# Seven products in place of eight for layer 2's first keys and queries, earlier inversions in layer 0, and a weight load from two queues

## The chip, the core and the metric

The kernel runs on one core of one Trainium2 chip. The metric is the device time of one execution in microseconds (us). Before the change it is 2660.78 us, the median of three runs (2659.78 to 2661.41). The profiled execution took 2661.49 us, its trace spans 2659.6 us, and TensorE was granted 0.999 of its full clock over that span.

PE below is TensorE's matmul pipe, DVE is VectorE, ACT is ScalarE, POOL is GpSimd, SP is the engine that issues most DMAs. All engines run at once; each works through its own list of instructions, and an instruction waits until the tiles that it reads and the buffers that it writes are free.

## What is computed

Four layers are applied one after the other to `x` of shape (4, 512, 64, 64), in float32. The four images are independent. Cut to what matters here:

```python
# layer 0: attention over all 4096 positions of one image, 64 channels
t = einsum('oc,bchw->bohw', w_qkv, x)           # key, query, value: 64 channels each
attn = softmax(einsum('bdk,bdq->bkq', key, query), axis=1)
x = scale * einsum('oc,bchw->bohw', w_out, einsum('bdk,bkq->bdq', value, attn)) + x
# layer 1: 1x1, 3x3 and 1x1 convolutions; weights mixed from 8 experts by a router; ReLUs; residual
# layer 2: linear attention
Q = softplus(Wq x + bq);  K = softplus(Wk x + bk);  V = Wv x + bv     # Q, K: 64 channels
KV = einsum('bmn,bcn->bmc', K, V)
norm = 1 / einsum('bnm,bm->bn', Q, K.sum(-1) + 1e-6)
x = x + gamma * einsum('bnm,bmc,bn->bcn', Q, KV, norm)
# layer 3: project to 1024 channels; the second half is scanned along rows and columns,
# goes through a sigmoid and gates the first half; residual
```

## The kernel before

An image's 4096 positions are held as four "pairs" of 1024 positions, and a pair as four chunks of 128 channels; `x[p, c, n]` is one pair. `P` is 128, `NB` 512, `KC` 4, `NPAIR` 4, `D` 64, `NT` 32, `ROUND` 8, `RING` 12. PE follows the program's order throughout. DVE and ACT follow it inside `manual_schedule` blocks that name them; elsewhere a scheduler orders them when the program is built.

PSUM is given out by two tags: three buffers of 128x1024 (`pair_psum`) and two of 128x512 (`bank`). A product that asks for a buffer waits until the last reader of the buffer's old content is done.

```python
def pair_psum(name):
    return ps.tile([P, 2, NB], F32, tag="s", name=name, bufs=3)
def bank(name, shape=(P, NB)):
    return ps.tile(list(shape), F32, tag="acc", name=name)          # 2 buffers
```

Start: the weights of layer 0 come in one transfer on ACT's queue, the first image in 16 transfers of 512 KB on SP's queue. The projections of layer 0 already use Strassen's seven products; the first image has a step list of its own:

```python
nc.scalar.dma_start(wqkv_sb, wqkv_t)
...
if b == 0:
    first = ("zero v0:0 1:0 v0:1 1:1 seed v0:2 2:0 v0:3 2:1 c11 t5 v1:0 v1:1 5 t6 v1:2 v1:3 cp01 t7 6 e2 "
             "v2:0 v2:1 t4 7 e3 c22 tr01 n5 4 c21 n6 3 c12 n7 v2:2 v2:3 n4")
# a digit: that product; v: values; t, n: sums on DVE; c11: four copies of keys on ACT
```

Layer 0's attention. In each of 16 rounds PE makes eight score tiles `s`, ACT takes their exponentials, DVE adds them up in `acc`, and PE multiplies eight earlier ones with the values. When a pair of queries is through, PE sums `acc` over partitions (`den`), DVE inverts it, and four output products `y` follow, one in a round:

```python
def inverse_sums(pr):
    den = bank(...);  2 matmuls of ones with accs[pr]
    recs[pr] = block(...);  nc.vector.reciprocal(recs[pr], den)
def sums(pr, early=True):
    if early: inverse_sums(pr)
    o = avs[pr] * recs[pr]                     # DVE
    if early: sum_range(pr)                    # two reductions on DVE
def out_step(pr, m):                           # y = pair_psum(...), 2 matmuls; x += scale * y on DVE
    add_out(pr, m, out_product(pr, m))

for g in range(NPAIR * NT // ROUND):
    for i in range(g * ROUND, (g + 1) * ROUND):
        scores(i)
    ...
    while done < (g + 1) * ROUND - (RING - ROUND):
        if done == NPAIR * NT - 5:
            inverse_sums(NPAIR - 1)            # the last pair, ahead of its last values
        pr = values(done)
        done += 1
        if pr is not None:
            late.append((g, lambda pr=pr: sums(pr)))
            if pr < NPAIR - 2:
                late += [(g + 1, lambda pr=pr, m=m: out_step(pr, m)) for m in range(KC)]
    ...
    if late and late[0][0] <= g:
        late.pop(0)[1]()                       # one step of the waiting list in a round
```

Layer 1's last convolutions run into layer 2's first features:

```python
def conv3(pr, h2):
    for m in range(KC):
        y = pair_psum(f"c3_{b}_{pr}_{m}")
        for h in range(2):
            nc.tensor.matmul(y[:, h, :], wc[:, KC + 9 + m, :], h2[:, h, :], start=True, stop=True)
        xm = xs[pr][:, m, :]
        nc.vector.scalar_tensor_tensor(xm, flat(y), bn_s[:, 2 + m:3 + m], xm, ALU.mult, ALU.add)
        nc.scalar.activation(xm, xm, AF.Relu, bias=bn_t[:, 2 + m:3 + m])

def features(w, pair):                         # w = 1: keys, 0: queries; 16 matmuls of 64 columns
    z = pair_psum(f"z_{b}_{w}_{pair[0]}")
    for i in range(2):
        feature_part(w, pair, z, i, 0, KC)
    return lambda: softplus(w, pair, z)

def softplus(w, pair, z, in_parts=False):
    nc.scalar.activation(e, z, AF.Abs, ...)
    nc.scalar.activation(pos, z, AF.Relu, ...)
    nc.scalar.activation(e, e, AF.Exp, scale=-1.0)
    nc.vector.tensor_scalar(u, e, 1.0, None, ALU.add)
    nc.scalar.activation(ln, u, AF.Ln)         # then softplus_end:
    # DVE: u = (u - 1) - e;  pos = pos + ln;  two times k = pos - u (or q)

h2[2] = conv2(2)
conv3(1, h2[1])
h2[3] = conv2(3)
weights = load_quarters(b)
features(1, (0, 1))()()
conv3(2, h2[2])
...
rest = features(0, (0, 1))
with tc.manual_schedule(engines={mybir.EngineType.DVE}):
    key_transpose((0, 1))
    rest = rest()
    move(0, 0)                                 # xtr, by pair_psum; its copy on DVE
    move_by_halves(0, 1)
    conv3(3, h2[3])
    g = bank(f"g_{b}", (P, C))
    keys = features(1, (2, 3))
    rest()
    ...
```

Layer 3 works through step lists that interleave "s" (the half that is scanned), "g" and "h" (gates). The last image ends with a list of its own, in which `rows`, `columns`, `fourth`, `second` are DVE's, and `turn`, `sigmoid`, `copy_out`, `third`, `d` are ACT's:

```python
end_steps = (...,
    ("s7", "s copy_out 3", "l turn 0", "l columns 0", "l sigmoid 1"), ("s5", "s fourth"),
    ("s4", "s third", "d", "s rows 1", "l sigmoid 0"), ("g5",),
    ("s3", "s second", "s turn 1", "s rows 0"), ...,
    ("g7", "s sigmoid 1", "g copy_out 3", "g first", "g fourth"), ("h6", "h copy_out 2"),
    ("h2", "s sigmoid 0", "h first"), ...)
```

Of the kernel before, what the change touches and what calls it, by code (L numbers as in the profile page):

```python
# [8 lines left out]
F32 = mybir.dt.float32  # L9
AF = mybir.ActivationFunctionType  # L10
ALU = mybir.AluOpType
# [35 lines left out]
def unshifted(ctx: ExitStack, tc: tile.TileContext, fits, x, wqkv_t, wout_t, router_t,  # L47
# [13 lines left out]
# [4 lines that stand above are left out]
        return ps.tile(list(shape), F32, tag="acc", name=name)  # L65
# [4 lines left out]
    def block(name, shape=(P, NB)):  # L70
        return blkp.tile(list(shape), F32, tag="blk", name=name)
# [25 lines left out]


    wqkv_sb = const.tile([P, KC, 3 * D], F32, tag="wqkv", name="wqkv_sb")
    nc.scalar.dma_start(wqkv_sb, wqkv_t)  # L100
    prm_sb = const.tile([P, NPRM], F32, tag="prm", name="prm_sb")
    nc.scalar.dma_start(prm_sb, prm)
    def col(i, n=1):
# [109 lines left out]
    class Projections:  # L213
# [16 lines left out]
        def steps(self, b):  # L230
            first = "v1 cp01 5 1 seed v2a t6 2 c11 t4 n5 6 v2b e2 n6 7 e3 c22 tr01 n7 4 c21 3 c12 n4"
            if b == 0:

                first = ("zero v0:0 1:0 v0:1 1:1 seed v0:2 2:0 v0:3 2:1 c11 t5 v1:0 v1:1 5 t6 v1:2 v1:3 cp01 t7 6 e2 "
                         "v2:0 v2:1 t4 7 e3 c22 tr01 n5 4 c21 n6 3 c12 n7 v2:2 v2:3 n4")
            return first.split(), "5 1 seed v3a 2 c11 6 v3b e2 cp23 7 e3 c22 tr23 k 4 c21 3 c12".split()

# [109 lines left out]
    def layer0(b, xs, pro):  # L347
# [62 lines left out]
        def sums(pr, early=True):  # L410
            if early:
                inverse_sums(pr)
            av, rec = avs[pr], recs[pr]
            o = block(f"o_{b}_{pr}")
            if pr >= NPAIR - 2:
                i = pr - NPAIR + 2
                nc.vector.scalar_tensor_tensor(o, av, 1.0, rec, ALU.mult, ALU.mult, accum_out=osum[:, i:i + 1])
            else:
                nc.vector.tensor_tensor(o, av, rec, ALU.mult)
            outs[pr] = o  # L420
            if early:
                sum_range(pr)
# [31 lines left out]
        with tc.manual_schedule(engines={mybir.EngineType.Activation}):  # L454
# [3 lines that stand above are left out]
                if 1 < g < 2 + 2 * KC:  # L458
                    pool(NPAIR - 2 + (g - 2) // KC, (g - 2) % KC)
                if g == 1:  # L460
                    pro.key_copies()
                while done < (g + 1) * ROUND - (RING - ROUND):
                    if done == NPAIR * NT - 5:
                        inverse_sums(NPAIR - 1)
                    pr = values(done)
                    done += 1
                    if pr is not None:
                        late.append((g, lambda pr=pr: sums(pr)))
                        if pr < NPAIR - 2:
                            late += [(g + 1, lambda pr=pr, m=m: out_step(pr, m)) for m in range(KC)]  # L470
                if b == 0 and g == 1:
                    router = router_of_values()
                if b == 0 and g == 2:
                    router()
                if late and late[0][0] <= g:
                    late.pop(0)[1]()
        assert not late
# [61 lines left out]
    def layer1(b, xs, wcq, sel, rw, ex4, ex7):  # L539
# [98 lines left out]
                                     AF.Relu, bias=bn_t[:, 1:2], scale=bn_s[:, 1:2])  # L638
            return h2

        def conv3(pr, h2):
            for m in range(KC):
                y = pair_psum(f"c3_{b}_{pr}_{m}")
                for h in range(2):
                    nc.tensor.matmul(y[:, h, :], wc[:, KC + 9 + m, :], h2[:, h, :], start=True, stop=True)  # L645
# [3 lines that stand above are left out]
# [9 lines left out]
    def layer2(b, xs, sums_of_six, mix_last, conv2, conv3, wcq, qs):  # L658
# [14 lines left out]
        def features(w, pair):  # L673
# [4 lines that stand above are left out]
# [27 lines left out]
        def key_transpose(pair):  # L705
            ktr = pair_psum(f"ktr_{b}_{pair[0]}")
            for i, pr in enumerate(pair):
                for j in range(TPB):
                    nc.tensor.transpose(ktr[:, i, j * P:(j + 1) * P], kts[1, pr][:, j * P:(j + 1) * P], ident)
            kt = four(f"kt_{b}_{pair[0]}")  # L710
            nc.vector.tensor_copy(kt, ktr)
            for i, pr in enumerate(pair):
                kts[pr] = kt[:, i, :].rearrange("p (j c) -> p j c", c=P)
# [40 lines left out]
        with tc.manual_schedule(engines={mybir.EngineType.DVE}):  # L754
            sums_of_six(0)
            sums_of_six(1)
            sums_of_six(2)
            mix_last()
            h2 = {0: conv2(0)}
            sums_of_six(3)  # L760
            h2[1] = conv2(1)
            conv3(0, h2[0])
        h2[2] = conv2(2)
        conv3(1, h2[1])
        h2[3] = conv2(3)
        weights = load_quarters(b)
        features(1, (0, 1))()()
        conv3(2, h2[2])


        def invert(pair):
# [14 lines left out]
            q = qs[:, pair[0]:pair[1] + 1, :]  # L786
            nc.vector.tensor_tensor(q, q, nrm, ALU.mult)

        rest = features(0, (0, 1))
        with tc.manual_schedule(engines={mybir.EngineType.DVE}):  # L790
            key_transpose((0, 1))
            rest = rest()
            move(0, 0)
            move_by_halves(0, 1)
            conv3(3, h2[3])
            g = bank(f"g_{b}", (P, C))
            keys = features(1, (2, 3))
            rest()
            keys = keys()
            products(0, ahead(1))  # L800
            keys()
            products(1, ahead(2))
            kfold = bank(f"kfold_{b}", (P, NPAIR))
            nc.tensor.matmul(kfold, fold, ks, start=True, stop=True)
            ksum = small.tile([P, 1], F32, tag="ksum", name=f"ksum_{b}")
            nc.vector.tensor_reduce(ksum, kfold, AX.X, ALU.add)
            for h in range(2):
                r = slice(h * D, (h + 1) * D)
                nc.vector.tensor_scalar(kbd[r, 16 * h:16 * (h + 1)], ones[r, 0:16], ksum[r, :], 1e-6, ALU.mult, ALU.add)
            key_transpose((2, 3))  # L810
            inv = invert((0, 1))
            products(2, ahead(3))
            divide((0, 1), inv)
            weights[2]()
            products(3)
            g_sb = block(f"gsb_{b}", (P, C))
            nc.scalar.copy(g_sb, g)
            gt = block(f"gt_{b}", (P, KC, P))

            late = (0, (2, 3), pair_psum(f"z_{b}_0_2"))  # L820
            feature_part(*late, 0, 0, 2)

            gk = pair_psum(f"gk_{b}")
            for kc in range(KC):
                nc.tensor.matmul(gk[:, 0, kc * P:(kc + 1) * P], g_sb[:, kc * P:(kc + 1) * P], fold,
                                 start=True, stop=True)
            nc.scalar.copy(gt, gk[:, 0, :].rearrange("p (kc c) -> p kc c", c=P))
            feature_part(*late, 0, 2, 2)
            kv = small.tile([P, C], F32, tag="kv", name=f"kv_{b}", bufs=1)
            for i in range(2):  # L830
                part = slice(i * C // 2, (i + 1) * C // 2)
                kvp = bank(f"kvp_{b}_{i}", (P, C // 2))
                for kc in range(KC):
                    nc.tensor.matmul(kvp, gt[:, kc, :], wv_sb[:, kc, part], start=kc == 0, stop=kc == KC - 1)
                nc.vector.scalar_tensor_tensor(kv[:, part], bv_sb[:, part], ksum, kvp, ALU.mult, ALU.add)
# [41 lines left out]
    def layer3(b, xs, value_product, value_add, left, weights, wcq):  # L877
# [109 lines left out]
        class Gates(Block):  # L987
# [32 lines left out]
            def add_x(self, i, h=None):  # L1020
# [24 lines left out]

        end_steps = (("s1", "s seed", "l rows 1", "l rows 0"), ("g1", "g seed"),
                     ("s6", "s copy_out 2", "l turn 1", "l columns 1"), ("s2", "s first"),
                     ("s7", "s copy_out 3", "l turn 0", "l columns 0", "l sigmoid 1"), ("s5", "s fourth"),
                     ("s4", "s third", "d", "s rows 1", "l sigmoid 0"), ("g5",),
                     ("s3", "s second", "s turn 1", "s rows 0"), ("g6", "g copy_out 2"),  # L1050
                     ("g2", "s turn 0", "s columns 1"), ("h1", "h seed", "s columns 0"),
                     ("g7", "s sigmoid 1", "g copy_out 3", "g first", "g fourth"), ("h6", "h copy_out 2"),
                     ("h2", "s sigmoid 0", "h first"), ("g4", "g third"), ("g3", "g second"),
                     ("h7", "h copy_out 3"), ("h5", "h fourth"), ("h4", "h third"), ("h3", "h second"))
        pro = None
        ys = [(pr, m) for pr in range(1, NPAIR) for m in range(KC)]
# [523 lines left out]
```

## Time and profile before

| engine | busy us | share of the span | instructions |
|---|---|---|---|
| PE | 2637.0 | 99% | 10050 |
| PE's weight loads | 1117.6 | 42% | 10050 |
| DVE | 2019.8 | 76% | 2272 |
| ACT | 1315.4 | 49% | 1510 |
| POOL | 11.0 | 0% | 26 |

A float32 matmul appears as two records in this trace, so a product of four matmuls is "x8". A record's own duration (some 590 ns for 512 columns) overlaps with its neighbours; what a record costs is the distance from one start to the next. The chain view lists the work that ended last, with those distances: 32 records of a 128x128 tile took 6.87 us there, 0.215 us each. Records of 64-column matmuls, which run two side by side in the halves of the array, have the same mean distance: 32 of them, layer 2's features, took 7.02 us.

The DMA queues moved 115.17 MB, 43 GB/s over the span; the busiest stretch is the start, with 404 to 416 GB/s from 6 to 22 us.

### The profile page before, as it was taken

To read this page: it belongs to the slowest core of one execution; us is meant where nothing else is said; L and a number is where in the kernel's file an instruction comes from. 1 tells how busy PE (TensorE), PEld (TensorE's weight loads), DVE (VectorE), ACT (ScalarE), POOL (GpSimd) and SP (SyncE) were. 2 spreads that over 40 slices of the span, in tenths; PEclk is the share of its full clock that TensorE was granted. 3 is DMA by queue.
4 is the path that set the end of the run, shared out by engine and by line. 5 is a ranking of instruction groups with operands and counts; after the bars stand their busy time and mean duration, and the time that the engine had idled before them with its cause. 6 is when DMAs were issued, how large, how long until landed. Compare 5 with 4: busy or idle time off the path is not lost.

```text
span 2659.6 us, 25807 instructions
## 1 busy us (share of the span) xinstructions
PE 2637.0 (99%) x10050; PEld 1117.6 (42%) x10050; DVE 2019.8 (76%) x2272; ACT 1315.4 (49%) x1510; POOL 11.0 (0%) x26
## 2 busy tenths in 40 slices
PE   9999999999999999999999999999999999999998
PEld 3333464444333345444433334544443333554443
DVE  6777866888777786688877778668887777856887
ACT  4555353454555435345556552535555554263545
POOL 1000000000000000000000000000000000000000
PEclk9999999999999999999999999999999999999999
DMA  5000210022200021012220002101121000210001
GB/s 192 1 1 1 103 32 1 24 103 80 79 1 1 1 103 32 1 42 84 79 80 1 1 2 102 32 1 63 64 94 65 0 1 24 80 32 1 32 40 57
DMA packets 34595, 115.17 MB, mean 43 GB/s; under 512 B 3104, under 2 KB 11808, under 8 KB 32928
## 3 DMA queue, kind: packets, MB, share of 16 engines
q1 hardware_dynamic: 34176, 113.01, 11.4%
q8 instruction: 81, 1.33, 0.2%
q14 instruction: 50, 0.41, 0.0%
q10 hardware_dynamic: 288, 0.42, 0.0%
HBM read 79.86 MB, written 33.55 MB: 43 GB/s over the span
## 4 chain that ended last, share of the span: by engine, by line
PE 96%; DVE 2%; issue 1%; ACT 1%; DMA 0%; DVEq 0%; ACTq 0%
PE sx L929 16%; PE av L389 16%; PE s L374 16%; PE zy L929 12%; PE z L670 4%; PE c L645 4%; PE c L573 4%; PE c L622 3%; PE wv L847 2%; PE y L433 2%; PE kq L310 2%; PE vv L263 2%; PE g L748 2%; PE xtr L733 2%; PE kqz L310 2%; PE c2e L622 2%
## 5 line engine op out<-in xcount | busy, mean ns | idle before, releaser
L374 PE MATMUL s<-qv,key 64*128 64x512 f32 x2048 | 453.8, 593 | 0.0
L377 ACT ACTIVATE ring<-s 128x1024 f32<-128x1024 f32 x336 | 315.4, 1051 | 249.7 <-PE s L374 249.7
L382 DVE TENSOR_TENSOR acc<-acc,ring 128x1024 f32<-128x1024 f32 x312 | 381.7, 1223 | 52.6 <-ACT ring L377 24.3
L389 PE MATMUL av<-ring,qv 128*64 128x512 f32 x1344 | 302.7, 596 | 0.0
L374 PEld LDWEIGHTS s<-qv,key 64*128 64x128 f32 x2048 | 192.8, 186 | 253.7 <-issue 111.4
L929 PE MATMUL sx<-t,x 128*128 128x512 f32 x512 | 232.4, 593 | 0.0
L377 ACT ACTIVATE x<-s 128x1024 f32<-128x1024 f32 x176 | 166.7, 1054 | 127.1 <-PE s L374 127.1
L382 DVE TENSOR_TENSOR acc<-acc,x 128x1024 f32<-128x1024 f32 x168 | 205.5, 1223 | 30.7 <-ACT x L377 14.2
L389 PEld LDWEIGHTS av<-ring,qv 128*64 128x64 f32 x1344 | 92.6, 137 | 200.1 <-issue 200.1
L934 ACT COPY zy<-sx 128x512 f32<-128x512 f32 x64 | 36.5, 570 | 254.0 <-PE sx L929 253.9
L389 PE MATMUL av<-x,qv 128*64 128x512 f32 x704 | 160.7, 599 | 0.0
L979 DVE TENSOR_TENSOR_SCAN t<-x,t 128x512 f32<-128x512 f32 x128 | 149.1, 1209 | 1.6
L929 PEld LDWEIGHTS sx<-t,x 128*128 128x128 f32 x512 | 96.7, 190 | 124.6 <-issue 121.2
L938 ACT ACTIVATE e<-sx,prm_sb 128x512 f32<-128x512 f32 x128 | 87.9, 687 | 122.7 <-PE sx L929 122.7
L962 DVE TENSOR_TENSOR_SCAN s<-wc,s 128x512 f32<-128x512 f32 x128 | 146.1, 1202 | 0.0
L968 ACT COPY t<-s 128x1024 f32<-128x1024 f32 x64 | 127.4, 1990 | 29.5 <-DVE s L962 29.0
L985 ACT ACTIVATE s<-t 128x1024 f32<-128x1024 f32 x64 | 125.8, 1991 | 11.1 <-DVE t L979 11.1
L929 PE MATMUL zy<-t,wq 128*128 128x512 f32 x256 | 118.5, 602 | 0.0
L929 PE MATMUL zy<-x,wq 128*128 128x512 f32 x256 | 118.0, 600 | 0.0
L929 PE MATMUL zy<-x,x 128*128 128x512 f32 x256 | 116.4, 594 | 0.8 <-DVE s L951 0.8
L929 PE MATMUL sx<-x,wq 128*128 128x512 f32 x256 | 117.1, 595 | 0.0
L929 PE MATMUL sx<-t,wq 128*128 128x512 f32 x256 | 116.6, 595 | 0.0
(227 smaller groups left out, 3455.6 us busy)
## 6 DMA issues: line engine op xcount, KB each, us to landing
out_dram<-s SPq DMA_DIRECT2D x62, 512.0 KB, 2.6
x<-in_x_dram SPq DMA_DIRECT2D x12, 2048.0 KB, 8.6
x<-in_x_dram SPq DMA_DIRECT2D x16, 512.0 KB, 8.9
ex<-in_packed_dram SPq DMA_DIRECT2D x4, 2048.0 KB, 7.7
ex<-in_experts_dram SPq DMA_DIRECT2D x4, 2048.0 KB, 7.9
wq<-in_wproj_t_dram SPq DMA_DIRECT2D x32, 256.0 KB, 5.1
ex<-in_packed_dram SPq DMA_DIRECT2D x4, 1536.0 KB, 6.0
ex<-in_experts_dram SPq DMA_DIRECT2D x4, 1536.0 KB, 6.4
```

The source lines that it names most:

```text
L310: nc.tensor.matmul(to[h * D:(h + 1) * D, :], self.w[k][:, c, :], self.term(xs, pair, k, c)[:, h * NB:(h + 1) * NB], start=c == 0 and k in ...
L374: nc.tensor.matmul(s[:, h, :], key[r, kt * P:(kt + 1) * P], qry[r, pr * NB:(pr + 1) * NB], start=True, stop=True)
L377: nc.scalar.activation(p, s, AF.Exp)
L382: nc.vector.tensor_tensor(accs[pr], accs[pr], p, ALU.add)
L389: nc.tensor.matmul(avs[pr][h * D:(h + 1) * D, :], vt[:, kt, :], ring[i % RING][:, h, :], start=kt == 0, stop=kt == NT - 1)
L573: nc.tensor.matmul(y[:, h, :], wc[:, kc, :], xs[pr][:, kc, h * NB:(h + 1) * NB], start=kc == 0, stop=kc == KC - 1)
L622: nc.tensor.matmul(y[:, lo - a:hi - a], u, v[:, lo:hi], start=dy == 1, stop=dy == 2)
L929: nc.tensor.matmul(y, w[:, c, self.kind, self.j * P:(self.j + 1) * P], v[:, c, :], start=c == 0 and k in (1, 5), stop=c == 1, skip_group_c ...
L962: nc.vector.tensor_tensor_scan(self.half(i, h), along[:, self.j + 2 * i, :], self.half(i, h), 0.0, ALU.mult, ALU.add)
L968: nc.scalar.copy(self.t[i].rearrange("p (w r) -> p w r", w=W), self.s[i].rearrange("p (r w) -> p w r", w=W))
L979: nc.vector.tensor_tensor_scan(th, down[:, i, :], th, 0.0, ALU.mult, ALU.add)
L985: nc.scalar.activation(self.s[i].rearrange("p (r w) -> p w r", w=W), tw, AF.Sigmoid)
```

## The change

It has four parts.

1. Layer 2's keys and queries of pairs 0 and 1 come from one run of Strassen's seven products over (keys, queries) x (pair 0, pair 1), where two `features` calls made eight. It needs sums of weights and of inputs on DVE, three copies on ACT, and sums of the results on DVE. The four outputs of `conv3(2)` are put between the products to give the other engines time. The keys' softplus moves behind the last product, the transposition of the keys behind `conv3(3)`.
2. In layer 0, `sums` of a finished pair is done in the round in which its values end, and no longer waits its turn in the list `late`.
3. At the start, `wqkv` comes in two halves, one on ACT's queue and one ahead of the first image on SP's; and product 5 goes ahead of the key copies and the second pair's values.
4. At the end, `l columns 0` and `l sigmoid 1` go behind `s fourth`, and `s sigmoid 0` goes one step forward.

The diff, cut to its core:

```diff
-    nc.scalar.dma_start(wqkv_sb, wqkv_t)
+    for queue, k in ((nc.scalar, 0), (nc.sync, 2)):
+        queue.dma_start(wqkv_sb[:, k:k + 2, :], wqkv_t[:, k:k + 2, :])
...
-                first = ("zero v0:0 1:0 v0:1 1:1 seed v0:2 2:0 v0:3 2:1 c11 t5 v1:0 v1:1 5 t6 v1:2 v1:3 cp01 t7 6 e2 "
+                first = ("zero v0:0 1:0 v0:1 1:1 seed v0:2 2:0 v0:3 2:1 t5 5 c11 v1:0 v1:1 t6 v1:2 v1:3 cp01 t7 6 e2 "
...
+                ended = None
                 while done < (g + 1) * ROUND - (RING - ROUND):
...
                     if pr is not None:
-                        late.append((g, lambda pr=pr: sums(pr)))
+                        ended = pr
...
+                if ended is not None:
+                    sums(ended)
                 if late and late[0][0] <= g:
                     late.pop(0)[1]()
...
-        def conv3(pr, h2):
-            for m in range(KC):
+        def conv3(pr, h2, ms=range(KC)):
+            for m in ms:
...
+        def first_features(between):
+            xa, xb = ((x[:, 0:2, :], x[:, 2:4, :]) for x in xs[0:2])
+            t5, t6 = (xsum[:, i:i + 2].rearrange("p c h n -> p c (h n)") for i in (0, 2))
+            ...                                   # four sums of weights on DVE: w5, w6, w7, w3
+            ws = {1: a11, 2: a12, 3: w3, 4: a22, 5: w5, 6: w6, 7: w7}
+            ts = {1: xa[0], 2: xa[1], 3: xb[1], 4: t5, 5: t5, 6: t6, 7: t6}
+            zy, y = pair_psum(f"zz_{b}"), bank(f"zs_{b}")
+            def product(k): ...                   # 4 matmuls, to y for k in (1, 6, 7, 4), else to zy
+            sub(t5, xb[0], xa[0]); sub(t6, xb[1], t5)          # each sub: two DVE operations
+            yield
+            product(5); product(1)
+            nc.scalar.copy(zy[:, 0, :], y)
+            sub(t5, xa[1], t6)
+            between(0)
+            product(2); product(6)
+            e2 = copy_out(2)
+            between(1)
+            sub(t6, xb[1], xb[0])
+            between(2)
+            product(7)
+            e3 = copy_out(3)
+            between(3)
+            zq = xsum[:, 2]
+            nc.vector.tensor_tensor(zq[:, 1, :], zy[:, 1, :], e3, ALU.add)
+            product(4)
+            nc.vector.tensor_copy(zq[:, 0, :], y)
+            product(3)
+            nc.vector.tensor_tensor(zy[:, 1, :], zy[:, 1, :], e2, ALU.add)
+            yield zy, zq
...
         conv3(1, h2[1])
+        xsum = bigp.tile([P, 4, 2, NB], F32, tag="big", name=f"xsum_{b}")
+        first = first_features(lambda m: conv3(2, h2[2], (m,)))
+        next(first)
         h2[3] = conv2(3)
         weights = load_quarters(b)
-        features(1, (0, 1))()()
-        conv3(2, h2[2])
+        zk, zq = next(first)
+        keys = softplus(1, (0, 1), zk)
...
-        rest = features(0, (0, 1))
         with tc.manual_schedule(engines={mybir.EngineType.DVE}):
-            key_transpose((0, 1))
-            rest = rest()
             move(0, 0)
             move_by_halves(0, 1)
+            keys()
             conv3(3, h2[3])
+            key_transpose((0, 1))
+            rest = softplus(0, (0, 1), zq)
...
-                     ("s7", "s copy_out 3", "l turn 0", "l columns 0", "l sigmoid 1"), ("s5", "s fourth"),
+                     ("s7", "s copy_out 3", "l turn 0"), ("s5", "s fourth", "l columns 0", "l sigmoid 1"),
...
-                     ("g7", "s sigmoid 1", "g copy_out 3", "g first", "g fourth"), ("h6", "h copy_out 2"),
-                     ("h2", "s sigmoid 0", "h first"), ...
+                     ("g7", "s sigmoid 1", "g copy_out 3", "g first", "g fourth"), ("h6", "s sigmoid 0", "h copy_out 2"),
+                     ("h2", "h first"), ...
```

## The prediction

> **What bounds the kernel now.** I read the page's first part, then the waits of PE, then the chain, then the timeline of the stages that the change touches.
>
> ```profile
> PE 2637.0 (99%) x10050; PEld 1117.6 (42%) x10050; DVE 2019.8 (76%) x2272; ACT 1315.4 (49%) x1510; POOL 11.0 (0%) x26
> ```
>
> PE is the bound nearly everywhere: 22.6 us of the span are without a matmul, and most of them lie at the two ends. The waits of PE (what it waited for, total us, times, longest) say what is left to win without taking matmuls out:
>
> ```profile
> PE den L405 <- DVE acc L382: 8.9, 4, 2.2
> PE kqz L303 <- POOL ident masks.py:199: 1.5, 1, 1.5
> PE vv L263 <- DMA wqkv_sb<-in_wqkv_t_dram: 1.0, 1, 1.0
> PE kqz L310 <- ACT key L293: 0.8, 1, 0.8
> PE zy L929 <- DVE s L951: 0.8, 1, 0.8
> ```
>
> Each image loses 2.2 us before the last pair's `den`; the start loses 1.0 and 0.8, the end 0.8. The change aims at each of these. The chain, in order of time, for layer 2's entry (start, us, what):
>
> ```profile
> 371.56 2.54 PE c2e L622 x12
> 374.10 7.02 PE z L670 x32
> 381.12 7.06 PE c L645 x16
> 388.18 7.02 PE z L670 x32
> 395.20 1.02 PE ktr L709 x8
> 396.22 0.87 PE xtr L733 x8
> 397.09 0.87 PE xtr L724 x8
> 397.97 6.87 PE c L645 x16
> ```
>
> It is PE alone: nothing waits here. A run of one shape costs 6.87 us; going from whole tiles to 64-column ones costs 0.15 us more (7.02), going back 0.19 (7.06).
>
> **What the Trainium skill says.** Three places bear on this. *PSUM — Partial Sum Buffer*, Specifications: 8 banks of 512 float32 in a partition. Three buffers of two banks and two of one are all eight, so a result that is held longer leaves the products fewer buffers. *Perfetto Trace Analysis*, Tensor Engine Instruction: DVE and ACT are strict FIFO; the timeline of before shows them in program order, so a DVE operation whose input is late holds up all behind it. *TensorE: Matmul & The Clock Gate*, Part 1: an idle window of about 3.4 us can halve PE's clock until it has been busy for as long. The trace shows the slow state at the start (four records from 6.27 to 8.03 us, 0.44 us each, against 0.215 later), and none after the waits of 2.2 us.
>
> **The change, part by part.** Beside before's trace I use the list of the changed program, which names what every instruction waits for. PE's order is the same in all four images.
>
> *Layer 2, matmuls.* 32 matmuls (64 records, 2 x 7.02 us) become 28. A product of layer 0's same scheme takes 1.72 us in the chain, seven 12.04. Without shape changes the old pair costs 14.04 - 0.30 = 13.74, so 1.7 us is saved. But the conv outputs between the products raise the entries into 64 columns from two to four and the returns to conv tiles from one to three: 2 x (0.15 + 0.19) = 0.7. Net -1.0 us an image.
>
> *Layer 2, DVE and ACT.* DVE gets four weight sums (0.29 as the 128x128 sums at the start), eight sums of 1024 (1.22 as layer 0's), three PSUM operations of 512 (0.69): 13 us an image, 52 in all, 78% busy. Before, DVE sits idle for 4.4 us ahead of `dq` and 7.5 us in the first features, so most of it fits. I walked PE, ACT and DVE through with these durations; up to the last product every input is there in time (closest: the seed copy, done 0.5 us ahead of product 2).
>
> *Layer 2, the keys.* Here I expect a new wait. Before, the keys are complete as `conv3(2)` begins, and their softplus runs under its 7 us. After, they are complete only with the last product, product 3; their softplus stands in DVE's list ahead of the additions of `conv3(3)`. These rows of before's timeline (start, duration) give the pitch of that chain:
>
> ```profile
> 381.17 1.11 ACT L683 ACTIVATE sp<-z,prm_sb 128x1024 f32<-128x1024 f32 x1 [3.03 <-PE z L670]
> 382.18 1.11 ACT L684 ACTIVATE pos<-z,prm_sb 128x1024 f32<-128x1024 f32 x1
> 383.17 1.06 ACT L685 ACTIVATE sp<-sp 128x1024 f32<-128x1024 f32 x1
> 384.27 0.69 DVE L686 TENSOR_SCALAR sp<-sp 128x1024 f32<-128x1024 f32 x1
> ```
>
> From product 3's end: DVE adds e2 (0.1 + 0.7), ACT does abs, relu and exp (1.0 + 1.0 + 1.1), DVE adds one (0.7), ACT takes the logarithm (1.05), DVE forms u, pos and two k (1.2 + 1.1 + 2 x 0.6), then adds the first output of `conv3(3)` (1.3): 10.7 us with the hand-overs. In that time PE has 1.9 us of transpositions and three outputs of 1.72. Each output needs one of three buffers. The third takes the buffer of `xtr`, whose copy on DVE stands behind "adds one" and ends at 5.8 us; PE is there at 5.3, a wait of 0.5. The fourth takes the first's, free at 10.7; PE is there at 7.5, a wait of 3.1. So +3.6, with -1.0: **+2.6 us an image, +10.4 in all**. Behind it the queue of DVE is some 3 us later against PE than before, which its idle 5.2 us ahead of the next softplus takes in.
>
> *Layer 0, the last `den`.* Before, DVE inverts pair 2's sums (3.36 us), multiplies and reduces (2.0) inside the last round, among the eight additions; the last addition ends 15.5 us after the round's first score, and PE is at `den` after 13.3. After, all this is done two rounds earlier. Eight additions at a pitch of 1.30 us from 2.1 us on end at 12.7, so the wait goes: **-8.9 us**.
>
> *Layer 0, the rounds that take it.* The inversion now stands ahead of the addition of an output product of the same round (pair 0's last with pair 1's inversion, pair 1's last with pair 2's). That product holds a PSUM buffer. The inversion starts 0.84 us before the round's first score and lasts 3.3; the addition ends at 3.7 us. The round's fourth score tile needs that buffer and would be due at 2.66; the third now needs the first's exponential, at 2.27 in place of 1.77. Net 1.1 us, twice an image: **+8.7 us**.
>
> *Start and end.* Product 5 ahead of the key copies saves the 0.8 us wait; t5 is done at 14.1 us, PE is there at 15.6. The first matmul needs half of `wqkv` and the first chunk of x. *DMA: Bandwidth & Descriptors*, Issuing engines are not separate DMA queues, says that both queues share the 16 engines; the trace agrees, with 415 GB/s already before the first matmul. The same bytes come first, so I give this 0.2 us. At the end `s fourth` ahead of the column scans saves 0.75, and the last sigmoid one step sooner 0.6 to 0.8; after that DVE works without a gap to the end, so both arrive. **-2.4 us** together.
>
> *The sum:* +10.4 - 8.9 + 8.7 - 2.4 = +7.8 us, 2668.6 us. I predict 2668.5.
>
> **The rivals.** First, *both waits stay away*: the matmuls saved, the `den` wait gone, and nothing comes for it. For it speaks that PE is the bound and that the change was built around idle engines; against it that the two waits follow from buffers and orders in the program. It would make -4 - 8.9 - 2.4, some 2645 us. Second, *the new wait in layer 2 cools the clock*: a wait of 3.1 us is near the 3.4 us window that the skill gives. Then the records behind it take twice as long for about 3.4 us: +1.7 an image, +7, some 2675 us. Against it: the wait is shorter than the window, and 2.2 us did nothing before. Third, *layer 0's gain is taken back wholly or doubly*: if DVE's lag from the early inversions reaches the next round too, each costs 2 us and not 1.1, some 2676 us; against it, a round has about 2.5 us of idle DVE ("2.54 <- PE y" ahead of an output's addition). Fourth, *one half of the loss is missing*: if only layer 2 waits, 2660; if only layer 0 does, 2654.
>
> **Range and chances.** The terms sum to nearly the time before, each with an error of one to three us: layer 2 +10.4 (7 to 14), the rounds +8.7 (4 to 12), `den` -8.9 (-9 to -6), ends -2.4 (-3 to -1). Added as if independent that is some 5 us to either side, with the clock and the lag on the upper side: 2661 to 2677. A move of 2% would be 53 us; no rival comes near, so within 2% gets 0.98.
>
> **What would show it.** In the changed profile: 10018 PE instructions, 32 fewer (16 matmuls); PE's waits without the four `den` entries of 2.2 us; four waits of about 3 us at `c` (conv3) for DVE's addition to x, and four of about 0.5; eight at `s` for DVE's addition of `y`, 0.6 to 1.1; no wait of kqz for key copies and none of zy for `s` at the end; each product of the new scheme at 1.72 us. Wrong would be: conv3 of pair 3 without a gap (the softplus is faster than its pitches say, or a buffer comes free in another order), score rounds without a gap, a new wait inside the seven products, or 64-column changes that cost more or less than 0.34 us a round trip.

## The result and the profile after

The changed kernel takes **2668.22 us** (median of 6 runs, 2667.71 to 2670.85) against 2660.58 us before (6 runs, 2659.78 to 2661.57). The ratio is 1.0031, with a 95% interval of 1.0018 to 1.0044: slower by 0.3%, 0.3 us under the predicted 2668.5. The sum was right, in part by luck: three of its terms were over 2 us too small, and their errors cancelled.

The first line of the page of the changed kernel, and then what PE waited for (total us, times, longest):

```profile
PE 2635.7 (99%) x10018; PEld 1113.3 (42%) x10018; DVE 2065.1 (77%) x2332; ACT 1323.1 (50%) x1522; POOL 12.1 (0%) x26
```

```profile
PE c L650 <- DVE x L652: 11.6, 4, 2.9
PE s L376 <- DVE x L440: 3.2, 8, 0.4
PE s L376 <- ACT ring L379: 2.1, 8, 0.3
PE c L650 <- DVE xt L740: 2.0, 4, 0.5
PE kqz L305 <- POOL ident masks.py:199: 1.5, 1, 1.5
PE xtr L738 <- DVE xt L740: 0.9, 4, 0.2
PE vv L265 <- DMA x<-in_x_dram: 0.6, 1, 0.6
```

Three waits that the change aimed at are gone: the four of `den`, that of `kqz` for the key copies, and that of `zy` at the end. In their place stand four waits of 2.9 and four of 0.5 us in `conv3` (L650), and eight pairs of short ones at the scores (L376). PE has 32 instructions fewer, as counted, but this list sums to 21.9 us of idle time where that of before sums to 13.9 (the lines that the prediction shows, and 0.9 of `xtr`).

The chain of layer 2's entry in the first image (start, us, what):

```profile
370.40 1.87 PE zz L787 x8
...
388.76 1.74 PE zz L787 x8
...
393.46 0.95 ACT sp L690
...
394.44 0.69 DVE sp L691
395.13 1.13 DVE xt L740
396.26 1.21 DVE sp L698
397.47 1.15 DVE pos L699
...
398.64 1.31 DVE k L703 x4
399.96 1.21 DVE x L652
...
401.21 3.65 PE c L650 x4
404.86 0.90 PE ktr L714 x8
```

Before, this stretch was PE alone. Now the chain leaves PE when the last product ends, goes through the softplus of the keys on ACT and DVE, and comes back at 401.21 with the fourth output of `conv3(3)`, 10.7 us after the last product: the predicted length to a tenth. What was not predicted is the 3.65 behind it. The same four records take 1.72 elsewhere. The timeline of the changed kernel shows that this did not happen in every image (start, us, instructions; in brackets the idle time before them and what ended it; first image, then the second):

```profile
396.32 1.98 PE L650 MATMUL c<-h,wc 128*128 128x512 f32 x4 [0.51 <-DVE xt L740]
401.21 3.65 PE L650 MATMUL c<-h,wc 128*128 128x512 f32 x4 [2.91 <-DVE x L652]
...
1065.12 1.98 PE L650 MATMUL c<-h,wc 128*128 128x512 f32 x4 [2.91 <-DVE x L652]
1066.94 1.04 PE L714 MATMUL ktr<-ident,k 128*128 128x128 f32 x8
```

The second image has the same wait, to a hundredth, and the matmuls behind it run at full speed; so do the third's and fourth's. (In the timeline a group's last record is counted to its modelled end, so a group of 1.72 stands as 1.98.)

### The profile page after: what moved, and what is told of

Its sections match the earlier page's. It is cut to its first block, busy times and chain, and to the rows that moved or that the text cites. A ratio compares the mean times of both kernels' runs of the same rounds, so it can differ in the third digit from the quotient of the medians.

```text
span 2666.0 us, 25839 instructions
## 1 busy us (share of the span) xinstructions
PE 2635.7 (99%) x10018; PEld 1113.3 (42%) x10018; DVE 2065.1 (77%) x2332; ACT 1323.1 (50%) x1522; POOL 12.1 (0%) x26
## 4 chain that ended last, share of the span: by engine, by line
PE 95%; DVE 3%; ACT 1%; issue 0%; DMA 0%; SPq 0%; ACTq 0%
PE av L391 17%; PE sx L991 16%; PE s L376 16%; PE zy L991 12%; PE c L578 4%; PE c L650 4%; PE c L627 3%; PE wv L909 2%; PE z L675 2%; PE vv L265 2%; PE kq L312 2%; PE y L435 2%; PE g L753 2%; PE xtr L738 2%; PE kqz L312 2%; PE c2e L627 2%
## 5 line engine op out<-in xcount | busy, mean ns | idle before, releaser
L376 PE MATMUL s<-qv,key 64*128 64x512 f32 x2048 | 458.0, 594 | 5.3 <-DVE x L440 3.2
L376 PEld LDWEIGHTS s<-qv,key 64*128 64x128 f32 x2048 | 192.1, 186 | 263.9 <-issue 118.1
L650 PE MATMUL c<-h,wc 128*128 128x512 f32 x256 | 118.8, 607 | 13.7 <-DVE x L652 11.6
```

The costliest lines, as they stand in the source:

```text
L376: nc.tensor.matmul(s[:, h, :], key[r, kt * P:(kt + 1) * P], qry[r, pr * NB:(pr + 1) * NB], start=True, stop=True)
```

## The experiments

Ten kernels were run. Each is the changed kernel with one edit or two, and each has its own runs of the kernel before beside it (medians of 2660.9 to 2661.4 us). The times of kernels that keep the wait of 2.9 us scatter over 3 to 6 us, for a reason that the third and fourth experiments show.

### Layer 2 as it was

```diff
-        first = first_features(lambda m: conv3(2, h2[2], (m,)))
-        ...
-        zk, zq = next(first)
-        keys = softplus(1, (0, 1), zk)
+        features(1, (0, 1))()()
+        conv3(2, h2[2])
...
+        rest = features(0, (0, 1))
...
```

> The changed kernel with layer 2's first keys and queries by the 64 plain matmul instructions again. Theory (layer 2 costs 3.8 us an image, of which the clock 1.9): 15 us less, about 2653 us. Rival (layer 2 costs the 2.6 us of the prediction and the rest lies elsewhere): 10.4 us less, about 2658 us.

Measured: 2655.03 us (2654.09 to 2656.00), ratio to before 0.9976 (0.9966 to 0.9986). Layer 2's part costs 13.2 us, and everything else in the change, taken together, gains. The theory's amount (15) had the slow clock in all four images; by the profiles, which are 13.3 us apart, it was in one. From the start of the first product to the features of the last pairs takes 30.74 us in every image before, and after the change 35.37 in the first and 33.67 in the three others: 4.6 + 3 x 2.9 = 13.4.

### Matmuls in the wait

```diff
-            conv3(3, h2[3])
+            conv3(3, h2[3], range(3))
+            spare = bank(f"spare_{b}")
+            for _ in range(4):
+                nc.tensor.matmul(spare, ident, h2[3][:, 0, :], start=True, stop=True)
+            conv3(3, h2[3], (3,))
```

> Four matmuls of 512 columns, whose result nothing reads, stand in PE's list between the third and the fourth output of conv3(3) in each image, so PE has work in the first 1.7 us of the wait of 2.91 us; the wait for DVE's addition still ends at the same time. Theory (the idle stretch lets PE's clock drop, and the four records after it run at half speed): the output after the wait takes 1.72 us again in place of 3.65, 1.93 us less an image, 7.7 in all, about 2660.5 us. Rival (the slow output comes from DVE and ACT working on PSUM and SBUF beside it, or from leaving a long wait, whatever PE did in it): it stays at 3.65 and the time at 2668.

Measured: 2667.67 us (2666.48 to 2669.03), 0.6 us less than the changed kernel and not 7.7. Both theories missed, because the expectation was badly made: it rested on the first image alone, and took a matmul of this kernel for one record of 0.43 us where it is two. (A record that uses the whole array takes 0.43 us: `c L645 x16` in the prediction's chain is 16 records in 6.87 us, not 32 as the section on the profile before has it. Only the 64-column records, two side by side, come to 0.22.) The four filled 3.43 us, more than the wait. In the first image the output behind them took 1.72 again and the stretch became 1.4 us shorter; in the other three, where nothing had been slow, it became 0.3 longer. The run by itself tells nothing of the cause.

### The output product ahead of the inversion

```diff
-                if ended is not None:
-                    sums(ended)
                 if late and late[0][0] <= g:
                     late.pop(0)[1]()
+                if ended is not None:
+                    sums(ended)
```

> In layer 0 the round's output product and its addition stand ahead of the inversion of the pair that has ended. Theory (the score tiles wait because the output's PSUM buffer is held while DVE inverts): the waits of s for DVE's addition to x go and those for the exponential behind them, 5.3 us in all: about 2663 us, the last den still without a wait. Rival (DVE's 3.4 us of inversion delay its additions to the sums, whichever stands first): the waits only change their place, about 2668 us.

Measured: 2666.90 us (2665.16 to 2670.41), ratio 1.0022 (1.0014 to 1.0030). By its time the rival holds: almost nothing came. The list of waits says otherwise: all sixteen waits of the scores are gone. The gain went to the wait in layer 2. Timeline of this kernel, the output of `conv3` behind that wait in the four images:

```profile
400.05 2.50 PE L650 MATMUL c<-h,wc 128*128 128x512 f32 x4 [2.91 <-DVE x L652]
...
1062.41 2.68 PE L650 MATMUL c<-h,wc 128*128 128x512 f32 x4 [2.91 <-DVE x L652]
...
1724.78 2.86 PE L650 MATMUL c<-h,wc 128*128 128x512 f32 x4 [2.91 <-DVE x L652]
...
2387.51 3.39 PE L650 MATMUL c<-h,wc 128*128 128x512 f32 x4 [2.91 <-DVE x L652]
```

All four are slow: in each image the granted clock, as the trace records it, is 0.50 for 3.41 us, against one image of four in the changed kernel; some 5 us are lost where 5 to 6 were won. The half clock begins at 401.38, 1063.57, 1725.75 and 2387.94 us, which is 1.33, 1.16, 0.97 and 0.43 us behind the start of these groups: the clock falls *after* PE has resumed, at a moment that the wait does not set.

### The same, with two matmuls in the wait

```diff
...
+            for _ in range(2):
+                nc.tensor.matmul(spare, ident, h2[3][:, 0, :], start=True, stop=True)
```

> The kernel with the output product ahead of the inversion, whose profile showed half the clock behind the wait of 2.91 us in all four images, with two matmuls that nothing reads in that wait: PE works 1.7 us of it and idles 1.2. The wait still ends when DVE's addition ends. Theory (what slows the matmuls behind the wait is the clock, let down by the idle stretch): no stretch at half clock, each image 1.7 us shorter, about 2660 us. Rival (the matmuls behind the wait are slow for another reason, as DVE and ACT at work beside them): as without the two matmuls, 2667 us.

Measured: **2660.60 us** (13 runs, 2659.97 to 2662.73), 6.3 us less than without them; the theory said 2660. Timeline in the first image:

```profile
397.33 1.88 PE L858 MATMUL spare<-h,ident 128*128 128x512 f32 x4
400.40 1.98 PE L650 MATMUL c<-h,wc 128*128 128x512 f32 x4 [1.19 <-DVE x L652]
402.23 1.04 PE L714 MATMUL ktr<-ident,k 128*128 128x128 f32 x8
```

The wait ends at the same DVE addition, DVE and ACT do the same work beside it, and yet nothing is slow in any image. Work that nobody reads makes the kernel 0.24% faster. The clock is the cause.

The record of the clock also shows when a wait lets it fall. Nine times in the middle of the twelve profiles the clock is halved, each time for 3.41 us, and the changes of one profile are whole multiples of 3413.3 ns apart, to 0.002 of one: from 401.38 to 1063.57 us it is 194.00. So the clock is set at the ends of windows that lie on a grid. In these lines of the view by windows (from:to, us, PE busy; the granted clock is the third number from the end) the changed kernel's wait falls whole into one window in the first image and is divided between two in the fourth:

```profile
397.97:401.38 3.41, 0.50 (x2) 0.17 (x2) 3.38 (x7) 2.43 (x4) 0.15 (x1) 1.00 0.00 0
401.38:404.80 3.42, 3.42 (x5) 1.25 (x6) 2.16 (x2) 3.33 (x4) 0.00 (x0) 0.50 0.00 0
2387.94:2391.35 3.41, 1.49 (x4) 0.78 (x5) 3.41 (x7) 2.39 (x3) 0.00 (x0) 1.00 0.02 5
```

With the output product ahead of the inversion, the first image's window is one with more work in it, and still the clock falls:

```profile
397.97:401.38 3.41, 1.33 (x3) 0.68 (x4) 3.41 (x7) 2.39 (x4) 0.00 (x0) 1.00 0.00 0
401.38:404.79 3.41, 3.41 (x12) 2.04 (x12) 2.78 (x3) 3.37 (x4) 0.00 (x0) 0.50 0.00 0
```

In all twelve profiles the clock falls behind every window in which PE was busy for 1.33 us or less, as this view counts it (nine windows, 0.50 to 1.33), and behind none with 1.49 us or more. With the two matmuls, no window of a wait in layer 2 has less than 2.2 us of work. The Trainium skill, *TensorE: Matmul & The Clock Gate*, Part 1, has a window of 3413 ns that is "free-running", that is, not started by the kernel. The records agree: the grid lies differently against the start of the program from profile to profile, with its first window ending between 0.40 and 2.62 us behind it.

### The additions ahead of the softplus

```diff
-            keys()
             conv3(3, h2[3])
-            key_transpose((0, 1))
+            keys()
             rest = softplus(0, (0, 1), zq)
             g = bank(f"g_{b}", (P, C))
             keys = features(1, (2, 3))
+            key_transpose((0, 1))
```

> The keys' softplus stands behind the four additions of conv3(3) in DVE's list, and the transposition of the keys behind the features of pairs 2 and 3 in PE's. Theory (the waits come only from DVE's additions standing behind the softplus chain): the waits of 0.51 and 2.91 us and the slow output, 1.93, go in each image, 5.35 each, 21.4 in all; some 0.3 us an image comes for the transpositions between 64-column work: about 2648 us. Rival (DVE's work is only put off): the softplus ends at some 14.5 us after the last product in place of 10.7, and a wait of 1 to 2 us an image comes at the transposed keys or the moved tiles: 2653 to 2657.

Measured: 2666.54 us (2665.00 to 2668.29). The rival is nearer, and even it was too kind. The waits of PE in this kernel:

```profile
PE xtr L738 <- DVE xt L740: 6.9, 4, 1.7
PE c L650 <- DVE xt L740: 3.3, 4, 0.8
...
PE xtr L738 <- DVE kt L716: 1.8, 4, 0.4
PE xtr L738 <- ACT pos L689: 1.5, 4, 0.4
```

The 2.9 us are gone, and 3.4 us an image stand in place of the 3.4 of both waits, in four pieces (0.2 of it, at `xtr`, was there before). DVE's late softplus now meets the moved tiles, whose copies it also makes, and the transposed keys come so late that their copy and the last features hold buffers which the moved tiles want.

### Both orders mixed

```diff
-        keys = softplus(1, (0, 1), zk)
...
             move(0, 0)
+            keys = softplus(1, (0, 1), zk)
             move_by_halves(0, 1)
-            keys()
             conv3(3, h2[3])
-            key_transpose((0, 1))
-            rest = softplus(0, (0, 1), zq)
+            keys()
+            rest = softplus(0, (0, 1), zq, i=0)
             g = bank(f"g_{b}", (P, C))
-            keys = features(1, (2, 3))
+            z23 = pair_psum(f"z_{b}_1_2")
+            feature_part(1, (2, 3), z23, 0, 0, KC)
+            feature_part(1, (2, 3), z23, 1, 0, 2)
+            key_transpose((0, 1))
+            feature_part(1, (2, 3), z23, 1, 2, 2)
+            keys = lambda: softplus(1, (2, 3), z23)
```

> Layer 2 of the changed kernel in another order: on DVE the copy of the first moved tile ahead of the softplus's addition of one, the four additions of conv3(3) ahead of the rest of the softplus; on PE the transposed keys between the halves of the last pair's features, so that DVE's late work finds PE busy. Theory (the two waits are an order of DVE's list and can be had away without a new one): both waits, 3.42 us an image, go, two more changes of tile shape cost 0.3, and no stretch is left in which the clock can drop: about 2654 us, no wait of c for DVE, PE's waits in layer 2 under 0.3 us each. Rival (as in the run with the additions first, put-off DVE work comes back as waits of xtr for its copies): 2660 us or more.

Measured: 2652.44 us (2652.06 to 2653.50), ratio 0.9969 (0.9957 to 0.9981). The copy of the moved tile goes ahead of the softplus's addition of one, the additions of `conv3` ahead of its end, and the keys are transposed in the middle of the last features, when they are just done (`i=0` only names the scratch that the queries' softplus uses). No wait of `c` is left. This is 2.6 us under the kernel with plain products: that is what seven products in place of eight are worth here when nothing waits for them. The runs also draw together, to within 1.4 us.

### Both repairs

> The same order of layer 2, and in layer 0 the output product ahead of the inversion; start and end as in the changed kernel. Theory (the gains add, and no wait near 3 us is left for the clock): 5.3 us less than the kernel with layer 2's order alone, about 2649 us, under both kernels. Rival (the score rounds' gain does not come, as when the time of that change alone went from 2668.2 to 2666.9 only): 2653 us.

This is the last edit and that of the output product together. Measured: **2646.36 us** (2646.15 to 2646.74), ratio to before 0.9946 (0.9933 to 0.9960): 0.54% faster than the kernel before and 0.8% faster than the changed one. The reordered rounds give 6.1 us now that no wait takes them back. Its waits of PE:

```profile
PE kqz L305 <- POOL ident masks.py:199: 1.5, 1, 1.5
PE xtr L738 <- DVE xt L740: 1.0, 4, 0.2
PE vv L265 <- DMA x<-in_x_dram: 0.5, 1, 0.5
```

### The start: one queue, and the old place of product 5

```diff
-    for queue, k in ((nc.scalar, 0), (nc.sync, 2)):
-        queue.dma_start(wqkv_sb[:, k:k + 2, :], wqkv_t[:, k:k + 2, :])
+    nc.scalar.dma_start(wqkv_sb, wqkv_t)
```

> The changed kernel with wqkv loaded by one queue, as before. Theory (the start's 3.6 us are mostly the clock: a shorter gap behind the first four matmuls keeps it up): the gap is 1.0 us again, the first value and key products run at half speed until about 10 us, and product 5 starts near 15.5 us in place of 12.8: 2670 to 2671 us. Rival (the gap has nothing to do with it, the clock's state there is chance): 0.4 us more, 2668.6.

Measured: 2671.28 us (2668.75 to 2674.89), 3.1 us more; the interval of the ratio, 1.0030 to 1.0057, overlaps that of the changed kernel. The start is read better in the timelines. With one queue:

```profile
6.60 1.97 PE L264 MATMUL vv<-x,wqkv_sb 128*64 128x512 f32 x4 [1.35 <-DMA wqkv_sb<-in_wqkv_t_dram]
8.36 1.57 PE L311 MATMUL kq<-x,wqkv_sb 128*64 128x512 f32 x4
```

and in the changed kernel:

```profile
5.83 1.08 PE L265 MATMUL vv<-x,wqkv_sb 128*64 128x512 f32 x4 [0.58 <-DMA x<-in_x_dram]
6.71 1.06 PE L312 MATMUL kq<-x,wqkv_sb 128*64 128x512 f32 x4
```

With one queue the first group comes 0.77 us later and it and much of the next run at half speed; product 5 starts at 14.94 and not at 12.77 us. Both profiles with one queue (this and before) show the cold start with gaps of 1.35 and 1.03 us. In the ten profiles with two queues the gaps are 0.2 to 0.8 us, and the matmuls are at full speed by 7.6 us at the latest. The trace's list of clock changes says how far that is the gap's doing. The clock becomes full behind the first window with 2.81 us of work or more, and not behind those with 2.69 or less. In the kernel before, the window from 3.84 to 7.25 us holds the gap and 2.38 us of work, so PE stays slow for one window more, to 10.66. With both orders mixed, and two queues, the window from 3.81 to 7.23 holds 2.81, and the clock is released: there the shorter gap decides. In the changed kernel a window ended at 5.44 us, ahead of the first product: its start is warm by where the window fell, and not by the load.

```diff
-zero v0:0 1:0 v0:1 1:1 seed v0:2 2:0 v0:3 2:1 t5 5 c11 v1:0 v1:1 t6
+zero v0:0 1:0 v0:1 1:1 seed v0:2 2:0 v0:3 2:1 c11 t5 v1:0 v1:1 5 t6
```

> The changed kernel with product 5 behind the key copies again, weights by two queues. Theory (the order is worth the wait for the key copies alone): that wait of 0.8 us is back and the clock at the start is up as in the changed kernel: 2669.0 us. Rival (the order is what keeps the clock up): 2671 us.

Measured: 2669.50 us (2667.01 to 2670.84), 1.3 us more with overlapping ranges. The wait of 0.8 us for the key copies is back in the list, and the start is warm (full clock from 5.90 us): the order is worth its wait, and nothing more shows in the profile.

### The end

```diff
-("s7", "s copy_out 3", "l turn 0"), ("s5", "s fourth", "l columns 0", "l sigmoid 1"),
+("s7", "s copy_out 3", "l turn 0", "l columns 0", "l sigmoid 1"), ("s5", "s fourth"),
...
-("h6", "s sigmoid 0", "h copy_out 2"), ("h2", "h first")
+("h6", "h copy_out 2"), ("h2", "s sigmoid 0", "h first")
```

> The changed kernel with the steps at the end in their former order. Theory (the end's share is the prediction's 1.4 us): 2669.6 us, the wait of zy for s of 0.8 us back in PE's list. Rival (something else at the end covers it): 2668.2 us.

Measured: 2672.44 us (5 runs, 2670.47 to 2675.87), more than either theory. The time cannot be used for so small an edit while the wait of layer 2 is in the kernel: in the slower of these runs the mean granted clock is 0.996 to 0.997, in the changed kernel 0.998 to 0.999. Within the profile the end can be measured by itself. From the first product of the last image's `wv` to DVE's last instruction takes 221.22 us before, 219.86 after the change, and 221.23 here: 1.4 us, the theory's, with the `zy` wait of 0.8 back.

## Why the prediction was right, and where not

**Layer 2, matmuls: right.** -1.0 us an image was predicted; from the first product to the first transposition takes 20.08 us in place of 21.10. Entries and returns cost 0.15 and 0.19 as taken from before's chain.

**Layer 2, the keys: right in mechanism, the term too small.** The waits were put at 0.5 and 3.1 and are 0.51 and 2.91. Two things were missing from the sum. Each wait costs 0.26 us beyond its length, 0.5 for the two in every image (33.67 = 30.74 - 1.02 + 3.42 + 0.53): 0.16 because the last record before it, of 0.59 us, is not overlapped by the next, which in a run starts after 0.43, and 0.10 because the group behind it takes 1.82 and not 1.72. And in some images the clock falls. So +2.9 an image and +11.7 in all, where +10.4 stood, and 1.7 us more for each image in which the clock falls, one in the profile.

**The second rival came about in part** (one image in the profile, none to four in others). The prediction argues against it that the wait is shorter than the window, and that 2.2 us did nothing before. Neither holds: what counts is the work in one window, and one of the four waits at `den` before the change did let the clock fall. The timeline of the kernel before, second and last image, `den` and the sixteen records of `av` soon behind it:

```profile
943.54 1.08 PE L405 MATMUL den<-acc,ones 128*64 128x512 f32 x4 [2.21 <-DVE acc L382]
...
945.31 3.60 PE L389 MATMUL av<-x,qv 128*64 128x512 f32 x16
...
2262.23 1.08 PE L405 MATMUL den<-acc,ones 128*64 128x512 f32 x4 [2.22 <-DVE acc L382]
...
2264.51 4.78 PE L389 MATMUL av<-x,qv 128*64 128x512 f32 x16
```

In the last image the same wait let the clock fall: its window, from 2260.05 to 2263.46 us, holds 1.23 us of work, those of the other three images 1.68 or more. The records take 4.78 where 3.60 is usual, and some 1.7 us are lost in all.

**Layer 0, the rounds: right.** 1.1 us each was predicted, 8.7 in all; measured are 1.2 and 9.7. One such round (start, us; second image):

```profile
838.31 1.03 PE L407 MATMUL den<-acc,ones 128*64 128x512 f32 x4
839.27 1.13 PE L435 MATMUL y<-o,wout_sb 64*128 64x512 f32 x4
839.39 3.36 DVE L410 RECIPROCAL rec<-den 128x512 f32<-128x512 f32 x1 [2.71 <-PE den L407]
840.23 1.88 PE L376 MATMUL s<-qv,key 64*128 64x512 f32 x8
842.38 1.13 PE L376 MATMUL s<-qv,key 64*128 64x512 f32 x4 [0.27 <-ACT ring L379]
842.66 1.18 DVE L440 SCALAR_TENSOR_TENSOR x<-y,prm_sb,x 128x1024 f32<-128x1024 f32 x1
...
843.91 4.56 PE L376 MATMUL s<-qv,key 64*128 64x512 f32 x20 [0.40 <-DVE x L440]
848.40 7.09 PE L391 MATMUL av<-ring,qv 128*64 128x512 f32 x32
```

The output `y` is made just ahead of the scores; DVE inverts for 3.36 us first and adds it only at 842.66. The third score tile waits for an exponential, the fourth for `y`'s buffer, as the walk had it. From the first score to `av` takes 8.17 us, in a usual round 6.96. The waits alone, 0.67, understate the loss by almost half: the rest, 0.27 a wait, comes on top of the waits as in layer 2. The prediction's net 1.1 left this out and put the waits themselves higher, at 0.6 to 1.1 for the one at `y`'s buffer alone, where 0.40 was measured.

**Layer 0, the last `den`: right.** From the last round's first score to `den` takes 13.12 us in place of 15.51: -2.4 an image, -9.6 in all, where -8.9 was put down (the wait alone). The last image gains another 1.7, the clock that no longer falls there. Rounds and `den` cancel: both, with the same matmuls, were set by where 3.4 us of inversion stand in DVE's list.

**The start: the step that failed.** -1.0 was predicted, 0.8 for the key copies and 0.2 for the load; product 6 starts at 17.92 and not at 21.56 us, -3.6. The key copies gave their 0.8 and 0.2 beyond it, and the load 0.4. The other 2.2 are the clock: the working saw half speed at the start of before, and took it as given. Part of that is chance, since the changed kernel's profile was released ahead of its first product. **The end: right,** -1.4.

By the profiles: -3.6 (start) + 9.7 (rounds) - 9.6 - 1.7 (`den`) + 13.4 (layer 2) - 1.4 (end) = +6.8; the spans differ by 6.4. The predicted +7.8 came from the same terms, with a start 2.6 too small and a layer 2 some 3 us too small. The `den` was 2.4 too small and the rounds 1.0 as well. Most of these errors is one thing, PE's clock: 2.2 us at the start, 1.7 in layer 2, 1.7 behind the last `den`. That they cancelled, and the total came within 0.3 us, is luck.

## What to carry to other kernels

On a kernel bound by PE, count a wait as its length, plus 0.2 to 0.3 us, plus a risk of 1.7 us if it is over some 2 us: fill it with anything, even work that nobody reads, or break it up, so that no window of 3.4 us is left nearly empty. When operations are moved into idle time of another engine, walk that engine's list in order, and ask which result PE will want next whose buffer stands behind the newcomer; here two changes of order turned a loss of 0.3% into a gain of 0.5% with the same arithmetic. And look at a repeated wait in all its occurrences before saying what it does or does not do.

## What the runs showed of the hardware

- PE's clock is set at the ends of windows of 3.41 us on a fixed grid. It was halved behind every window with 1.33 us of work or less and behind none with 1.49 or more; at the start it became full behind windows with 2.81 us or more and not behind those with 2.69 or less. The Trainium skill, *TensorE: Matmul & The Clock Gate*, Part 1, speaks of an idle window of about 3.4 us; here a window with up to 1.33 us of work counted as idle.
- So an idle stretch of 2.9 us, and even one of 2.2, can halve the clock for 3.41 us, and the same stretch a few hundred us later may not. One of 1.2 us did nothing in any image of the kernel with two matmuls in the wait.
- The half clock begins up to 1.3 us after PE has resumed work (401.38 against 400.05 us above), so the records that suffer need not be the first behind the wait.
- Whether it falls depends on time lost elsewhere: taking 5 us out of layer 0 moved the waits of layer 2 so that four of four were slow in place of one. A single edit's time is then no measure of that edit, and the profile's own stretches are.
